# When a block's transposes and its expert stand between the products of the way out

## The chip, the cores and the metric

The kernel runs on one core of one Trainium2 chip. The metric is device time in microseconds (us) of one execution. Each core has five engines that run side by side, each through its own instructions in order: TensorE (PE, matrix products), VectorE (DVE), ScalarE (ACT), GpSimd (POOL) and SyncE (SP, which here only issues transfers). They wait for one another through semaphores. Products are written to PSUM, 8 banks of 2 KB per partition; everything else lies in SBUF or in device memory.

## The reference, cut to what matters

A transformer layer on 32 sequences of 64 tokens of width 512, in float32: cross attention to 256 context tokens, causal latent attention with 16 heads, and a feed-forward part. The change touches the end of the attention and one branch of the feed-forward:

```python
x = x + (heads @ wo.T + wo_b)                       # the way out of the attention
h = layernorm(x)
up = square(relu(h @ up_w)); shared = up @ down_w   # 512 -> 2048 -> 512
moe = (h @ expert_weight) * top2_sum(h @ gate_w)    # one expert, scaled per token
x = x + layernorm(shared + moe) * gamma + beta
```

## The kernel before

Every float32 operand is split into a high and a low part (`split`, L138 to L143: ACT casts the high part, DVE subtracts for the low part), and a product is made of three matmuls (high x high, low x high, high x low). The large products are, on top of that, tiled by a scheme with seven products in place of eight: sums of quarter blocks go in, seven products come out, and `combine` (L152 to L163) adds these into the result.

**The way out** (its loop is `for u, (blk, k) in enumerate(out_units)`, L1003 on) has 8 blocks of 256 tokens and 64 units. A unit is one block with one of 8 weight slots `k`: `seven` (L692 to L705) issues 21 matmuls of 128x256 on PE, into the block's four PSUM banks. Blocks 0 and 1 share the first 16 units. From block 2 on, block b has units 8b to 8b+7, so blocks 3, 4, 5, 6 end with units 31, 39, 47, 55, and block 7 with 63. The four banks of blocks 2 to 7 come from one pool with a single buffer; a block writes the banks that the block before it used.

What surrounds a unit:

- `left(u + 2)` splits the operand of the unit after next: an ACT cast (L141) and a DVE subtraction (L143), 128x896 each, from a piece `c` into one of three `hl` buffers. A buffer comes free when the unit three back is done on PE.
- `read_pair` (L666 to L681) fetches the pieces `c` by SP (L680), into three buffers.
- At a block's last unit `combine` runs: an ACT copy from bank 0 (L154), then on DVE L156 (bank 1), L158 and L159 (banks 2 and 0), L160 (bank 2) and L162 (bank 3). Their result `oo` has one buffer.
- `o_sum` (L920 to L929) adds the residual `ox` (L922) and takes the statistics (L926, L927); a power on POOL (L121) ends the norm's factor; `o_norm` applies it (L133) and yields `on`.
- `o_t` (L951 to L974), the block's **transposes**: 8 on PE (L959, tile `ops`), then casts on ACT (`oh`), subtractions on DVE (`ol`), copies `oT`, two stores `xT` issued by ACT (L971). Behind it `o_beta` (L945 to L949) adds beta to `oo` on DVE (L948) and stores it (`x2d`, by SP). Only then is the buffer `oo` free.
- `o_expert` (L976 to L998), the block's **expert**: 48 matmuls on PE (tile `cpe`, L173 to L175) into four banks of a pool of their own, the sum of the two largest gate values on DVE (L990, L992), the scaling on ACT (L995, L996) and a store `mo` issued by ACT.
- In the last eight units the first weights of the next stage are fetched (`cw_up`), cast and split (`wh_up`, `wl_up`; DVE 128x1024 and 128x768).

**What sets the order.** The kernel is written as one program; a scheduler then places each instruction on its engine, by costs and dependencies that it estimates, and may move an instruction past its neighbours (`issue_after` pins one behind another). Where a block's transposes and its expert are written is set by two tuples, L55 and L56: transposes of block i follow unit `TURN_AT[i]`, its expert follows unit `MULT_AT[i]`. The built order follows the tuples but for the ends, where matmuls trade places: after unit 23, for example, 17 of block 1's 48 expert products stand ahead of unit 24.

```python
TURN_AT = (19, 22, 28, 34, 42, 50, 58)
MULT_AT = (21, 25, 31, 39, 47, 55, 63)
...
        if u in TURN_AT:
            i = TURN_AT.index(u)
            xT[i] = o_t(i, xns.pop(i))
...
        if u in MULT_AT:
            i = MULT_AT.index(u)
            scaled = o_expert(i, *xT.pop(i))
```

Block 7's transposes and expert follow the loop. Before, the experts of blocks 2, 3, 4 and 5 thus stand behind the last units of blocks 3, 4, 5 and 6.

Of the kernel before, what the change touches and what calls it, by code (L numbers as in the profile page):

```python
# [51 lines left out]

SLOT_AT = (3, 5, 7, 9, 11)
EXPERT_AT = (15, 16, 17, 18)
TURN_AT = (19, 22, 28, 34, 42, 50, 58)  # L55
MULT_AT = (21, 25, 31, 39, 47, 55, 63)  # L56

BETA_AT = 60

# [20 lines left out]
def perceiver_block(ctx: ExitStack, tc: tile.TileContext, x, mem, mask, wq_a, bq_a, qnw, wq_b, bq_b,  # L80
# [97 lines left out]
    with ExitStack() as mla:  # L178
# [409 lines left out]
        with ExitStack() as pb:  # L588
# [46 lines left out]
            def load_slot(k, what):  # L635
                put_slot(k, what, read_slot(k, what))
# [308 lines left out]
    def o_beta(blk, pin=None):  # L945
        o2 = x2s.pop(blk)
        with after(pin):
            nc.vector.tensor_tensor(o2, o2, beb.unsqueeze(1).to_broadcast([P, 2, D]), ALU.add)  # L948
        nc.sync.dma_start(x2_d[blk], o2)  # L949

    def o_t(blk, xn, between=None):  # L951
        xT = ap.tile([P, NKD, TB], FP, tag="xn", name=f"oT{blk}")
        xh = ap.tile([P, NKD, TB], FR, tag="xh", name=f"oh{blk}")
        xl = ap.tile([P, NKD, TB], FR, tag="xl", name=f"ol{blk}")
        turned = []
        for tt in range(2):
            ps = ps_t.tile([P, NKD, P], FP, tag="T", name=f"ops{blk}_{tt}")
            for k in range(NKD):
                nc.tensor.transpose(ps[:, k, :], xn[:, tt, k * P : (k + 1) * P], ident)  # L959
            sl = slice(tt * P, (tt + 1) * P)  # L960
            low = split(xh[:, :, sl], xl[:, :, sl], ps)[1]
            if between:
                turned.append((sl, ps))
            else:
                copy = nc.scalar.copy(xT[:, :, sl], ps)
        if between:
            between()
        for sl, ps in turned:
            copy = nc.scalar.copy(xT[:, :, sl], ps)
        for i in range(2):  # L970
            nc.scalar.dma_start(xT_d[blk // 2][:, i, blk % 2], xT[:, 2 * i : 2 * i + 2, :])  # L971
        if blk > 1 and blk != NB - 2:
            o_beta(blk, low)
        return xh, xl, (copy, low)  # L974

    def o_expert(blk, xh, xl, _):  # L976

        mo = mos.pop(blk, None) or ap.tile([P, 2, D], FP, tag="mo", name=f"mo{blk}")
        for tt in range(2):
            i = 2 * blk + tt  # L980
            sl = slice(tt * P, (tt + 1) * P)
            pes = []
            for c in (slice(256, NE), slice(0, 256)):
                pe = ps_t.tile([P, D], FP, tag="T", name=f"cpe{i}_{c.start}")
                mm3(pe[:, 0 : c.stop - c.start], [
                    (xh[:, k, sl], xl[:, k, sl], wes[0][:, k, c], wes[1][:, k, c]) for k in range(NKD)
                ])
                pes.append(pe)
            t8 = sp.tile([P, 8], FP, tag="t8", name=f"t8{i}")
            nc.vector.max(t8, pes[0][:, 256:264])  # L990
            gs = sp.tile([P, 1], FP, tag="gs", name=f"gs{i}")
            nc.vector.tensor_tensor(gs, t8[:, 0:1], t8[:, 1:2], ALU.add)  # L992
            if tt:
                yield
            nc.scalar.mul(mo[:, tt, 256:512], pes[0][:, 0:256], gs)  # L995
            nc.scalar.mul(mo[:, tt, 0:256], pes[1][:, 0:256], gs)  # L996
        nc.scalar.dma_start(mo_d[blk], mo)
        yield  # L998
# [4 lines left out]
    for u, (blk, k) in enumerate(out_units):  # L1003
# [28 lines left out]
        if u - 8 * (NB - 1) in (0, 2, 4, 6):  # L1032
            load_slot(ORDER[(u % 8) // 2], "up")
# [3 lines that stand above are left out]
# [11 lines left out]
        if u == BETA_AT:  # L1048
            o_beta(NB - 2, low[1])
# [3 lines that stand above are left out]
# [327 lines left out]
```

## Time and profile before

| what | us |
|---|---|
| runs: median of three (lowest, highest) | 1113.07 (1111.52, 1113.95) |
| the profiled execution | 1114.92 |
| its span, first to last instruction | 1113.1 |
| PE busy in the span | 1069.7 |
| the way out's products, first to last | 554.9 to 765.2 |
| its transposes, first to last | 619.9 to 776.0 |
| its experts, first to last | 621.8 to 784.0 |

The page gives one execution. In its rows PE, DVE, ACT and POOL are the engines, PEld is the loading of weights into PE. A timeline row reads: start in us from the span's start, duration, engine, source line, operation, output<-input, and in brackets how long the engine was idle before it and what ended the wait. A row of the chain of waits has a start, a length and what the time went to. Rows of stretches give PE's busy time, its instructions, the clock granted to PE (1.00 is full speed), the busy share of the 16 DMA engines and what they moved.

### The profile page before, as it was taken

Reading aid. Unit: us, or ns where it says so; the run is one execution under the profiler, and the core shown is the slowest. Engines: PE = TensorE matmul, PEld = TensorE weight load, DVE = VectorE, ACT = ScalarE, POOL = GpSimd, SP = SyncE. Lnnn points to the kernel's source line nnn. Section 1 sums busy time; section 2 is a strip of 40 time slices with the busy share of each in tenths; the row PEclk is TensorE's granted clock in tenths of the full one; section 3 lists DMA queues with packets and bytes.
Section 4 is the critical chain, followed back from the end, with each engine's and each line's share of the span. In section 5 each row is a group of like instructions: output and inputs, shape, how many; then the busy total and the mean of one; then the engine's idle time right before and its main releaser. Section 6 shows DMA issues by size and latency. Waiting matters only on the chain.

```text
span 1113.1 us, 25983 instructions
## 1 busy us (share of the span) xinstructions
PE 1069.7 (96%) x10182; PEld 984.6 (88%) x10182; DVE 772.9 (69%) x1363; ACT 547.6 (49%) x1048; POOL 508.0 (46%) x694
## 2 busy tenths in 40 slices
PE   8899999999999999999989999998999998999896
PEld 6677777679999999999889999998999998999896
DVE  4666666647666667666878866668776577688796
ACT  4344444433444434433556544445676667564553
POOL 2333333326778777775471100002058770056761
PEclk9999999999999999999999999998999999999999
DMA  8777666343676787772498776776755789998681
GB/s 260 224 229 231 210 213 209 113 159 126 250 243 236 252 285 265 254 250 105 141 363 298 248 240 227 219 265 232 242 189 193 238 291 279 297 314 254 205 246 59
DMA packets 195386, 254.67 MB, mean 229 GB/s; under 512 B 18544, under 2 KB 140032, under 8 KB 195264
## 3 DMA queue, kind: packets, MB, share of 16 engines
q1 hardware_dynamic: 190848, 241.45, 66.1%
q10 hardware_dynamic: 3456, 8.39, 2.1%
q0 software_dynamic: 960, 3.18, 0.9%
q8 instruction: 80, 1.31, 0.5%
q14 instruction: 42, 0.34, 0.1%
HBM read 146.67 MB, written 106.30 MB: 227 GB/s over the span
## 4 chain that ended last, share of the span: by engine, by line
PE 59%; DMA 12%; DVE 11%; POOL 7%; issue 6%; ACT 4%; SPq 1%; DVEq 0%; POOLq 0%; ACTq 0%
PE up L1115 10%; PE pss L749 6%; PE psq L173 4%; PE psq L174 4%; PE psq L175 4%; PE psv L793 3%; PE op L702 2%; PE op L701 2%; PE op L699 2%; PE psc L367 2%; DMA cw_down<-wd_down 2%; DVE hl L143 2%; PE pse L173 2%; PE pse L175 2%; PE pse L174 2%
## 5 line engine op out<-in xcount | busy, mean ns | idle before, releaser
L731 DVE SCALAR_TENSOR_TENSOR qe<-pse,bqp,cq 64x256 f32<-64x256 f32 x256 | 123.8, 483 | 79.4 <-PE pse L175 73.3
L1115 PE MATMUL up<-xr,wh_up 128*128 128x256 f32 x896 | 154.8, 278 | 2.9 <-ACT up L154 2.9
L1115 PEld LDWEIGHTS up<-xr,wh_up 128*128 128x128 f32 x896 | 136.6, 190 | 3.1 <-ACT up L154 3.1
L701 PE MATMUL op<-wh_wo,hl 128*128 128x256 f32 x448 | 125.5, 280 | 4.8 <-DVE hl L143 4.7
L701 PE MATMUL dp<-wh_down,hl 128*128 128x256 f32 x448 | 124.9, 279 | 4.4 <-DVE hl L143 4.4
L143 DVE TENSOR_TENSOR hl<-c,hl 128x896 fp32r<-128x896 f32 x85 | 96.8, 1140 | 45.5 <-ACT hl L141 45.4
L699 PE MATMUL dp<-wh_down,hl 128*128 128x256 f32 x448 | 124.4, 278 | 1.5 <-DVE uo L159 1.5
L699 PE MATMUL op<-wh_wo,hl 128*128 128x256 f32 x448 | 125.5, 280 | 0.3 <-ACT hl L141 0.3
L702 PE MATMUL op<-wl_wo,hl 128*128 128x256 f32 x448 | 124.4, 278 | 0.1
L702 PE MATMUL dp<-wl_down,hl 128*128 128x256 f32 x448 | 124.4, 278 | 0.0
L1115 PE MATMUL up<-xr,wl_up 128*128 128x256 f32 x448 | 122.9, 278 | 0.0
L141 ACT CAST hl<-c 128x896 fp32r<-128x896 f32 x85 | 79.9, 943 | 76.0 <-PE op L702 33.2
L173 PE MATMUL psq<-qa_hi,qh 128*128 128x256 f32 x384 | 112.7, 294 | 0.0
L174 PE MATMUL psq<-qa_hi,ql 128*128 128x256 f32 x384 | 106.6, 278 | 0.0
L175 PE MATMUL psq<-qa_lo,qh 128*128 128x256 f32 x384 | 106.5, 277 | 0.0
L701 PEld LDWEIGHTS op<-wh_wo,hl 128*128 128x128 f32 x448 | 84.4, 188 | 6.5 <-DVE hl L143 6.4
L701 PEld LDWEIGHTS dp<-wh_down,hl 128*128 128x128 f32 x448 | 84.8, 189 | 5.1 <-DVE hl L143 5.0
L699 PEld LDWEIGHTS dp<-wh_down,hl 128*128 128x128 f32 x448 | 84.8, 189 | 1.7 <-issue 1.7
L699 PEld LDWEIGHTS op<-wh_wo,hl 128*128 128x128 f32 x448 | 84.2, 188 | 1.1 <-issue 0.7
L702 PEld LDWEIGHTS dp<-wl_down,hl 128*128 128x128 f32 x448 | 84.8, 189 | 0.0
L1115 PEld LDWEIGHTS up<-xr,wl_up 128*128 128x128 f32 x448 | 84.8, 189 | 0.0
L702 PEld LDWEIGHTS op<-wl_wo,hl 128*128 128x128 f32 x448 | 84.4, 189 | 0.3 <-DVE wl_wo L143 0.3
(227 smaller groups left out, 3152.8 us busy)
## 6 DMA issues: line engine op xcount, KB each, us to landing
c<-vd SPq DMA_DIRECT2D x58, 448.0 KB, 4.3
cx<-in_ctx SPq DMA_DIRECT2D x32, 512.0 KB, 4.6
vd<-vw SPq DMA_DIRECT2D x29, 512.0 KB, 3.8
hd<-uo SPq DMA_DIRECT2D x107, 128.0 KB, 3.4
hd<-uw SPq DMA_DIRECT2D x21, 512.0 KB, 3.0
dcw<-hd SPq DMA_DIRECT2D x18, 448.0 KB, 5.7
vd<-v SPq DMA_DIRECT2D x30, 256.0 KB, 3.3
c<-hd SPq DMA_DIRECT2D x17, 448.0 KB, 5.8
```

The source lines that it names most:

```text
L141: copy = nc.scalar.copy(hi, src)
L143: return copy, engine.tensor_tensor(lo, src, hi.bitcast(FP), ALU.subtract)
L173: nc.tensor.matmul(ps, ah, bh, start=(j == 0), stop=False)
L174: nc.tensor.matmul(ps, al, bh, start=False, stop=False)
L175: nc.tensor.matmul(ps, ah, bl, start=False, stop=(j == n - 1))
L699: first = nc.tensor.matmul(ps[s // 2][:, s % 2], h[:, a], wh[:, b], start=(k == 0 and s % 2 == 0), stop=False)
L701: nc.tensor.matmul(ps[s // 2][:, s % 2], l[:, a], wh[:, b], start=False, stop=False)
L702: ins = nc.tensor.matmul(ps[s // 2][:, s % 2], h[:, a], wl[:, b], start=False, stop=last)
L731: rope = nc.vector.scalar_tensor_tensor(qe[64 * a : 64 * a + 64, :], pe[r, :], bqp[r, p : p + 1], cq[r, a, :], ALU.add, ALU.mult,)
L749: nc.tensor.matmul(ps[64 * j : 64 * j + 64, pj, b, :], qs[2 * pj + j][a][:, sl], kT[:, a, kt], start=(a == 0), stop=(a == 1),)
L793: nc.tensor.matmul(o, kv[a, i, :], t[a, bp, :], start=True, stop=True)
L1115: nc.tensor.matmul(ps[s // 2][:, s % 2], w[:, i, kk], xr[b, 2 * kk + low][:, j], start=(first and m == 0), stop=(last and m == len(parts) ...
```

## The change

```diff
-TURN_AT = (19, 22, 28, 34, 42, 50, 58)
-MULT_AT = (21, 25, 31, 39, 47, 55, 63)
+TURN_AT = (19, 22, 28, 35, 43, 51, 58)
+MULT_AT = (21, 25, 30, 37, 45, 53, 63)
```

The transposes of blocks 3, 4 and 5 follow one unit later. The experts of blocks 3, 4 and 5 follow two units sooner, and that of block 2 one unit sooner. Between a block's transposes and its expert stand two units (for block 2: two in place of three; for blocks 3 to 5: two in place of five). No instruction is added, removed or resized. Blocks 0, 1, 6 and 7 keep their numbers, though the scheduler's order changes around block 6 too: in the built program its transposes stand 17 matmuls later, inside unit 59, and 4 of its 48 expert products stand ahead of the last products of block 7.

## The prediction

> **What bounds the kernel now.** First the page: TensorE (PE) is busy for 96% of the span.
>
> ```profile
> span 1113.1 us, 25983 instructions
> PE 1069.7 (96%) x10182; PEld 984.6 (88%) x10182; DVE 772.9 (69%) x1363; ACT 547.6 (49%) x1048; POOL 508.0 (46%) x694
> ```
>
> The change lies in the way out, whose products run from 554.9 to 765.2 us and whose experts end at 784. So next the busy time by stretches (length; PE busy and instructions; granted clock; DMA share; GB/s):
>
> ```profile
> 640.00:750.00 110.00, 110.00 (x945) 1.00 0.73 240
> 770.00:772.00 2.00, 1.26 (x11) 1.00 0.03 9
> 772.00:774.00 2.00, 0.00 (x0) 0.90 0.00 0
> 774.00:776.00 2.00, 1.54 (x8) 0.50 0.65 262
> ```
>
> Where the moved pairs stand, 640 to 750 us, PE never pauses: a product issues every 0.1135 us, a unit of 21 takes 2.385 us, an expert's 48 took 5.77 us (659.46 to 665.23). **No order of the same matmuls can gain there; it can only open gaps.** What can be lost shows in VectorE's (DVE) timeline at the end of block 4 (unit 39), where PE issued the block's last product at 685.51 and expert 3's first at 685.63:
>
> ```profile
> 684.91 1.09 DVE L143 TENSOR_TENSOR hl<-c,hl 128x896 fp32r<-128x896 f32 x1 [1.96 <-ACT hl L141]
> 685.92 0.68 DVE L156 TENSOR_TENSOR oo<-op,op 128x512 f32<-128x512 f32 x1
> 686.71 0.42 DVE L158 TENSOR_TENSOR oo<-oo,op 128x256 f32<-128x256 f32 x1
> 687.16 0.42 DVE L159 TENSOR_TENSOR oo<-oo,op 128x256 f32<-128x256 f32 x1
> 687.50 0.41 DVE L162 TENSOR_TENSOR oo<-oo,op 128x256 f32<-128x256 f32 x1
> 687.83 0.68 DVE L160 TENSOR_TENSOR oo<-oo,op 128x512 f32<-128x512 f32 x1
> ```
>
> These five sums read the block's four PSUM banks, and the next block writes the same four (their pool has one buffer): bank 1 is free after L156, bank 0 after L159, bank 3 after L162, bank 2 after L160. They end 3.0 us after the block's last product, and nobody waits: PE is in the expert, whose banks are others, until 691.4. **The expert behind a block's last unit is the cover of its combine.** The last view is the chain of waits at the end of the stage:
>
> ```profile
> 759.72 1.23 DVE oo L948
> 760.95 0.02 issue
> 760.97 5.82 DMA x2d<-oo
> ...
> 766.91 0.70 DVE oo L156
> ...
> 773.38 0.94 DVE on L133
> 774.33 0.14 issue
> ```
>
> Block 7's combine waits until block 6's sum, in the single buffer `oo`, is stored; its norm ends the last transposes' wait. PE idles 3.2 us up to 774.46 and then runs at granted clock 0.50 to about 780.4 (rows of 2 us further on show 0.89 from 780 to 782): 6.0 us at half speed, 3.0 us lost.
>
> **The change, part by part.** Nothing is added or removed: the 48 products of three experts (blocks 3 to 5, 144 in all) move two units up, block 2's 48 one unit up, and 8 transposes x 3 blocks (3 to 5) one unit down. Moved work costs nothing itself. What it issues moves along: ScalarE's (ACT) store of `mo` comes earlier, its two stores of `xT` one unit later; both are read far later. On SyncE's queue the built order has the read of a block's second piece `c` ahead of the `x2d` store instead of behind, and `ox` one place later; the next to need `ox` is a whole block away (25 us).
>
> *Cover lost at four block ends.* In the new order nothing stands on PE between the last unit of blocks 3, 4, 5, 6 and the next block's first product; the built order starts these on bank 1, then 0, 3, 2: the order in which combine frees them. Blocks 4 to 6, counted from T, the slot after the block's last product: the piece cast ahead of L156 starts when the unit before is done, 0.20 after the slot that follows it (667.82 against 667.62), so at T - 2.18; its DVE half starts 0.98 later (667.82 to 668.80), T - 1.20; L156 1.01 later (684.91 to 685.92), T - 0.19; it takes 0.68, PE wakes 0.05 later (569.43 + 1.08 to 570.56), and the first pair after a wait costs 0.11 more (570.56 to 570.78): **0.65 us of gap**. L159 starts 1.24 after L156 and ends at T + 1.47, when PE is still on bank 1 (9 products, to T + 1.7). Bank 0 costs nothing, the others follow.
>
> The trace has no block end without cover, so bounds from the nearest rows, T to the end of L156: 686.60 - 685.63 = 0.97 at block 4; block 2, whose next block came 17 expert products later, 635.03 - 633.29 = 1.74; block 6, 740.76 - 737.97 = 2.79; below, 0, if the cast is early. The large ones have a cause: the cast ahead of L156 had waited for its read (idle before it 2.11 us at 683.93 and 2.58 at 738.09, put down to DMA `c`). In the new order that read leaves ahead of the store, and 5.77 us of expert stand between its issue and its need. I take 0.65 and keep 0 and 2.8.
>
> At block 3 the built order puts the cast of unit 34 between L158 and L159, and it needs unit 31 done: ACT at T + 0.20, DVE T + 1.18 to 2.27, PE again 0.05 + 0.11 later; PE has 13 products (1.47 us) until it needs it: 0.95. Sum: 0.95 + 3 x 0.65 = **2.9 us**.
>
> *Block 6's queue.* With block 5's expert gone from behind unit 55, DVE meets the burst and the `up` weights together. From L156 at T - 0.19, by starts in the rows: L160 at 1.72, a cast 2.32, L922 3.32, first `wl_up` 4.47, two L926 to 6.82, second `wl_up` to 7.9, then the cast of unit 59, whose end is 9.04. PE gets there at 0.65 + 3 x 2.385 + 4 products = 8.25: 0.95 with the restart. Block 6's norm, now behind one more cast, then holds its transposes about 0.25. In the same units PE lost 0.43 + 0.16 + 0.60 = 1.2 us before (steps at 757.3, 759.9, 762.9); I leave that as it is, plus 0.15. Sum: **1.35 us**; ends 0 and 2.5 (twice the 1.2).
>
> *The end of the stage.* The build now has 4 of block 6's expert products ahead of the last unit, so PE reaches its last product later: 4 x 0.117 = 0.47. The beta sum L948 moves behind one more `wl_up` (0.87), and its store behind one more 512 KB read on SyncE (at the 339 to 430 GB/s of these slices 1.2 to 1.5). Before, the store landed at 766.79, 1.46 after the last product's next slot (765.33); now 0.9 to 2.3 later. I take 1.6. With the 0.47 this is **2.1 us**; from 0.5, if it lands under other DVE work, to 4. PE's idle time before the last transposes becomes some 5 us, and the half-speed stretch after it I leave at 3.0; half as long or half again as long, it would give 1.5 back or take 1.5.
>
> The total: 2.9 + 1.35 + 2.1 = +6.35 us. The profiled execution took 1114.92 us (span 1113.1, 1.8 around it), so its like would be 1121.3; it lies 1.85 above the median of the runs, 1113.07, to which the same difference gives **1119.4 us**.
>
> The trace has PE waits of 0.59 to 1.32 us between 570 and 590 with the clock at 1.00, so I charge no clock for the new gaps. A rule speaks otherwise. The Trainium skill, page "TensorE: Matmul & The Clock Gate", section "A second HAM failure mode: psum-queue depth-cycling", tells of a kernel whose short PE pauses at every change of PSUM banks made the clock swing between half and full. By that rule each of the four block ends could bring one 3.41 us window (the page's figure) at half rate, an estimate of 4 x 1.7 = 6.8 us more, 1126.2.
>
> **The rivals.**
> 1. *Late reads stay late*: each block end costs the 2.8 of block 6 and not 0.65 or 0.95. For it: the DMA share of 0.73, and idle times before casts that end on `c`. Against: the read now has an expert's time more. 4 x 2.8 - 2.9 = 8.3 more: 1127.7. Half of it, 1123.6, is likelier than all.
> 2. *The cover is not needed*: the casts run ahead, L156 ends before T, and DVE's burst at block 6 finds gaps. For it: DVE idles 31%. Against: a cast can't start before a buffer is free, and only three exist. Then only the 0.47 and some of the store: +1, 1114.1.
> 3. *Faster*: block 6's store gets out early. If `x2d` is issued before about 758.9 and not at 760.97, L156 starts 1.9 sooner, PE's idle time falls to the 1.3 us that left the clock alone at 570, and 3.0 of half clock go; with the 1.2 us of units 59 to 63 that is 6.1 less, against 2.9 more for the block ends: 1109.9. Against: the built order puts this store later on both of its queues.
>
> **How the numbers follow.** A measurement of this kernel tells 0.2% (2.2 us) from no change. Forecast, +4 to +9: 0.60. Only part of it, +2.2 to +4: 0.13. Late reads or clock, over +9: 0.15. Rival 2, within 2.2: 0.09. Rival 3: 0.03. So slower 0.88. The range from +2.4 to +11.9, 1115.5 to 1125.0, leaves out the two last cases and the far half of the late reads.
>
> **What will show it.** In the PE waits: three of about 0.5 us on `oo` L156 at block ends and one of about 0.9 on a cast (L143) 1.5 us after block 3's end; none in the expert or at the transposes of blocks 3 to 5. At unit 59 a wait on L143 of about 1 us. The chain's `x2d` piece again 5 to 7 us long, L156 2.5 to 4 us behind the last product and PE idle 4.5 to 6 us before the last transposes. I am wrong if PE stays gapless from 640 to 750, if the waits end on DMA `c`, or if the clock falls below 1.00 before the last transposes.

## The result, and the profile after

| | median of the runs, us (lowest, highest) | profiled execution | its span |
|---|---|---|---|
| before, 22 runs | 1113.58 (1108.51, 1117.92) | 1114.92 | 1113.1 |
| after, 22 runs | 1116.72 (1113.31, 1123.17) | 1113.31 | 1111.5 |

The ratio of all runs is 1.0035, with a 95% interval of 1.002 to 1.005: the change makes the kernel slower by 3.9 us (2.2 to 5.6); the two medians lie 3.1 us apart. The prediction was 1119.4 in a range of 1115.5 to 1125.0, so the sign and the range held, and the size was too large: the measured loss lies just below the main case (+4 to +9, 0.60), in the one that had 0.13.

One profile misleads here. The profiled execution after is shorter than the one before, although the kernel is slower: single executions scatter by some 10 us, and a profile is one of them. So I read the changed stage and not the span. First the page of the kernel after, its top lines:

```profile
span 1111.5 us, 25986 instructions
PE 1068.6 (96%) x10182; PEld 983.2 (88%) x10182; DVE 771.7 (69%) x1363; ACT 547.1 (49%) x1048; POOL 507.4 (46%) x694
```

The totals tell nothing: the work is the same. The stretch in which PE never paused before now has pauses, at a full clock. These rows show five engines, each with its busy time and instructions (PE, PEld, DVE, ACT, POOL), then the clock, the DMA share and GB/s:

```profile
640.00:750.00 110.00, 108.33 (x927) 107.52 (x926) 69.66 (x114) 49.22 (x73) 2.76 (x4) 1.00 0.71 232
```

Which they are, PE's waits in that stretch after say (what PE waits for; total us, times, longest us). The same view of before has no line at all:

```profile
PE op L699 <- DVE oo L156: 1.1, 3, 0.4
PE op L701 <- DVE hl L143: 0.5, 1, 0.5
```

The three waits on L156 are at the ends of blocks 4, 5 and 6, the one on a cast 1.6 us after block 3's end (664.5). The end of block 4 in VectorE's timeline of after; the last column is the idle time before an instruction and what ended it:

```profile
690.19 1.09 DVE L143 TENSOR_TENSOR hl<-c,hl 128x896 fp32r<-128x896 f32 x1 [4.42 <-ACT hl L141]
691.20 0.68 DVE L156 TENSOR_TENSOR oo<-op,op 128x512 f32<-128x512 f32 x1
691.99 0.42 DVE L158 TENSOR_TENSOR oo<-oo,op 128x256 f32<-128x256 f32 x1
692.44 0.42 DVE L159 TENSOR_TENSOR oo<-oo,op 128x256 f32<-128x256 f32 x1
```

And PE's timeline of the same place:

```profile
691.29 0.28 PE L702 MATMUL op<-wl_wo,hl 128*128 128x256 f32 x1
691.94 0.39 PE L699 MATMUL op<-wh_wo,hl 128*128 128x256 f32 x1 [0.38 <-DVE oo L156]
692.16 0.28 PE L701 MATMUL op<-wh_wo,hl 128*128 128x256 f32 x1
```

Block 4's last product issues at 691.29, so the next slot is 691.40. Block 5's first product waits for bank 1, which L156 leaves at 691.88, and issues at 691.94, 0.54 late; the next one takes 0.22 instead of 0.11. Together **0.65 us of gap**. The list of waits shows less (0.38), because it counts from the modelled end of the last product, not from the missed slot. L156 starts 0.20 before the slot; before, at the same place, it started 0.29 behind it (685.92 against 685.63), and nobody saw it, since 5.77 us of expert stood there.

The other half of the result is the end of the stage, in the chain of waits of after:

```profile
763.27 1.23 DVE oo L948
764.52 3.85 DMA x2d<-oo
768.50 0.70 DVE oo L156
...
774.97 0.94 DVE on L133
775.91 0.14 issue
776.05 0.64 PE ops L959 x4
```

The beta sum is 3.55 us later than before. Of this, 2.33 us are those by which the last product is later; against that product the sum is 1.22 us later, as its later place foretold, but the store takes 3.85 us and not 5.82. It lands at 768.37, 0.72 behind the slot after the last product (767.65); before it was 1.46. PE idles 2.95 us before the last transposes (3.19 before), and in this profile the half-speed stretch behind it is shorter too:

```profile
776.00:778.00 2.00, 1.57 (x10) 1.14 (x10) 1.44 (x2) 1.01 (x2) 2.00 (x3) 0.97 0.43 172
778.00:780.00 2.00, 1.93 (x8) 1.93 (x9) 1.82 (x3) 1.73 (x4) 2.00 (x4) 0.50 0.04 8
780.00:782.00 2.00, 2.00 (x13) 2.00 (x13) 1.57 (x4) 1.27 (x2) 1.79 (x2) 0.68 0.79 293
```

### The profile page after: what moved, and what is told of

The parts are those of the page before. It is cut to its first block, busy times and chain, and to the rows that moved or that the text cites. A ratio compares the mean times of both kernels' runs of the same rounds, so it can differ in the third digit from the quotient of the medians.

```text
span 1111.5 us, 25986 instructions
## 1 busy us (share of the span) xinstructions
PE 1068.6 (96%) x10182; PEld 983.2 (88%) x10182; DVE 771.7 (69%) x1363; ACT 547.1 (49%) x1048; POOL 507.4 (46%) x694
```

## The experiments

**The theories.** C, the cover: what costs is that no expert stands behind a block's last unit, so PE meets the combine. D, the distance: what costs is that only two units lie between a block's transposes and its expert, so that casts, stores and norms of one block are packed together. A smaller question went along: whether the later transposes are harmless, and what sets the end of the stage.

So that the runs can be compared, each profiled execution is cut in two, by PE's timeline: the *queue*, from the first product behind block 1's expert to block 7's last product (798 products, 40 transposes, four experts; in after, e2, e4, e5 and e6 also 4 products of the fifth, 0.5 us, and in e11 12, 1.5 us), and the *tail*, from there to block 7's first transpose. The ratio has its own runs of the kernel before on the same chip beside it.

| kernel | waits at ends of blocks 3, 4, 5, 6, us | queue | tail | ratio (interval) |
|---|---|---|---|---|
| before | none | 121.20 | 9.25 | 1 |
| after | 0.54, 0.38, 0.38, 0.38 | 124.15 | 8.51 | 1.0035 (1.002 to 1.005) |
| e1 transposes alone | none | 119.74 | 9.08 | 1.0003 (0.9986 to 1.0021) |
| e2 experts alone | 0.54, 0.38, 0.38, 0.38 | 127.05 | 8.83 | 1.0066 (1.004 to 1.0093) |
| e4 one expert alone | block 6: 0.38 | 122.60 | 8.66 | 1.0026 (1.0009 to 1.0043) |
| e10 all but that expert | 0.58, 0.38, 0.38, none | 123.58 | 9.21 | 1.0024 (1.0006 to 1.0042) |
| e3 two units, all late | none, none, 0.18, 3.76 | 125.50 | 8.31 | 1.0049 (1.0029 to 1.0069) |
| e9 two units, but block 5 | none, none, 0.30, none | 121.40 | 8.87 | 1.0012 (0.9988 to 1.0035) |
| e7 half an expert as cover | none | 120.93 | 8.88 | 1.0004 (0.9988 to 1.002) |
| e5 fewer PSUM banks | as after | 125.04 | 8.85 | 1.0047 (1.0025 to 1.0069) |
| e6 a second bank 1 | 0.69, 0.20, 0.21, 0.20 | 124.05 | 9.63 | 1.0046 (1.0028 to 1.0064) |
| e8 e1, earlier store | none | 120.50 | 7.57 | 0.999 (0.9974 to 1.0007) |
| e11 after, earlier store | as after | 125.26 | 6.91 | 1.003 (1.001 to 1.0051) |
| e12 e8, last sums by halves | none | 120.19 | 6.92 | 1.0 (0.9982 to 1.0018) |

The ratios go with the queue, and hardly with the tail. The five kernels that can't be told from before (e1, e7, e8, e9, e12) have a queue of 119.74 to 121.40, 120.55 on average, so the 121.20 of before's own profile may be a slow one; after's queue lies 2.95 above the one and 3.6 above the other.

**e1 and e2: the halves of the change.** e1:

```diff
-TURN_AT = (19, 22, 28, 34, 42, 50, 58)
+TURN_AT = (19, 22, 28, 35, 43, 51, 58)
```

> Only the transposes of blocks 3 to 5 one unit later; the experts stay behind the blocks' last units, four units behind their transposes. Theory C (cover: what costs is that no expert stands between a block's last product and the next block's first): no PE wait on the combine (L156) at any block end, time within 1 us of the kernel before. Rival D (distance: what costs is that transposes and expert lie close together, so that their casts and scalings crowd ACT and DVE): one unit of the three that were taken away is gone, so about a third of the change's +3.9 us, +1.3 us.

Ratio 1.0003: the later transposes alone cost nothing that can be measured, and there is no wait from 640 us to block 7. e2:

```diff
-MULT_AT = (21, 25, 31, 39, 47, 55, 63)
+MULT_AT = (21, 25, 30, 37, 45, 53, 63)
```

> Only the experts sooner; the transposes stay where they were, so three units lie between. Theory C: the same four gaps at the ends of blocks 3 to 6 (one on the cast L143, three on L156 of about 0.4 us) and the pile-up at unit 59, so at least the change's +3.9 us; on top, block 3 to 5's norms are late by then, because their statistics queue behind casts of a block that started earlier: three waits of the transposes on L133 of about 1 us each, so +5 to +9 us over before. Rival D: three units between instead of two, so slower than before by less than the change, about +2.6 us, and no waits at block ends that the change did not have.

Ratio 1.0066, more than the whole change, though the two intervals overlap. PE's waits of e2 from 640 to 750 us:

```profile
PE ops L959 <- DVE on L133: 2.8, 3, 0.9
PE op L699 <- DVE oo L156: 1.1, 3, 0.4
PE op L701 <- DVE hl L143: 0.5, 1, 0.5
```

The last two lines are those of after: the experts bring them, whatever the transposes do. The first line is new. Without an expert behind a block's end the next units come 5.77 us sooner, and the transposes that follow the third of them now wait for their norm. In the whole change the transposes stand one unit later, and these 2.8 us are not there. **So the change is a loss in its experts and a repair in its transposes.**

**e4 and e10: one block end by itself.** e4 moves block 5's expert alone, e10 all but that one.

```diff
-MULT_AT = (21, 25, 31, 39, 47, 55, 63)
+MULT_AT = (21, 25, 31, 39, 47, 53, 63)
```

> Only block 5's expert is moved, from behind unit 55 to behind unit 53; everything else as before. Theory C: of the change's cost just the last block end's part: one wait on L156 of 0.4 us behind unit 55, the wait of unit 59 on a cast (L143) of about 0.6 us and of block 6's transposes of 0.4 us, and in exchange the waits at units 61 and 63 (0.16 and 0.33 us) gone: +1 to +3 us. If the four block ends each cost a quarter: +1.0 us and no wait at unit 59.

```diff
-TURN_AT = (19, 22, 28, 34, 42, 50, 58)
-MULT_AT = (21, 25, 31, 39, 47, 55, 63)
+TURN_AT = (19, 22, 28, 35, 43, 51, 58)
+MULT_AT = (21, 25, 30, 37, 45, 55, 63)
```

> The changed kernel with block 5's expert left behind unit 55. Theory C: block ends 3, 4 and 5 keep their waits (one on L143 of 0.55 us, two on L156 of 0.38), block 6's end and unit 59 have none, and block 6's transposes do not wait: +1 to +2 us over before, the change less the +2.9 us of the kernel with block 5's expert alone moved. If the four ends cost alike: +2.9 us.

In e4 the wait on L156 stands at the end of block 6 and nowhere else, and the ratio is 1.0026; in e10 there is a wait at all ends but that one, ratio 1.0024. Each wait at a block end follows its expert. One point of e10's expectation failed: at unit 59, where none was to be, PE waits 1.05 us for a cast (753.28), and the loss is 2.7 us and not 1 to 2. The two costs add to 1.005, the whole change has 1.0035: within their intervals, the same.

**e3 and e9: two units between, with the cover kept.** Experts as before, transposes drawn up to two units ahead of them. e3:

```diff
-TURN_AT = (19, 22, 28, 34, 42, 50, 58)
+TURN_AT = (19, 22, 29, 37, 45, 53, 58)
```

> Two units between transposes and expert for blocks 2 to 5 as in the change, but reached by moving the transposes later (after units 29, 37, 45, 53); the experts stay behind the blocks' last units. Theory C: no wait on L156 at block ends, time within 1.5 us of before. Rival D: two units between, so the change's +3.9 us.

The ratio, 1.0049, is what D asked for, but the trace is not: no wait at the ends of blocks 3 and 4, one of 0.18 us at the end of block 5, one of 3.76 us at the end of block 6. The chain of e3 there, then PE's timeline:

```profile
735.86 1.23 DVE oo L948
737.09 0.02 issue
737.10 8.59 DMA x2d<-oo
...
745.78 0.69 DVE oo L156
...
747.10 0.38 ACT mo L996
```

```profile
747.53 0.43 PE L699 MATMUL op<-wh_wo,hl 128*128 128x256 f32 x1 [3.76 <-ACT mo L996]
747.76 0.42 PE L701 MATMUL op<-wh_wo,hl 128*128 128x256 f32 x1
```

This is a third cause. Transposes so late put the beta sum behind them late, its store took 8.59 us, and until it has landed the one buffer `oo` can't take block 6's sums. L156 waited 4.3 us, the expert's scaling (L992, L995, L996) stood behind it, and the products behind that issue 0.21 us apart instead of 0.11, at half clock. So e9 leaves block 5's transposes at their old place:

```diff
-TURN_AT = (19, 22, 28, 34, 42, 50, 58)
+TURN_AT = (19, 22, 29, 37, 45, 50, 58)
```

> As the kernel with two units between by later transposes, but block 5 is left as it was (transposes after 50, expert after 55), since there a store of oo came too late and held PE for 3.8 us. Blocks 2 to 4 still have two units between. Theory C, with the store as the cause of that kernel's loss: no wait at any block end, from one expert's start to the next 26.2 us or a little less, time within 1 us of before. Rival D: three of the four close pairs stay, so about 3 us of the change's 3.9.

Its only wait from 640 to 750 us:

```profile
PE op L699 <- ACT mo L996: 0.3, 1, 0.3
```

Ratio 1.0012, no clear difference, with two units between for blocks 2, 3 and 4. The 0.3 us is e3's mechanism in small: block 4's store (711.45, 5.59 us) ends at 717.04 and L156 behind it. The ratio alone doesn't settle D: its interval still holds the 3 us that D asked for. The trace does: from one block's last product to the next block's, e9 takes 25.89 us for blocks 4 and 5, before 26.17. And e2, with three units between, lost 4.4 to 10.3 us where D asked for 2.6. **D falls**: two units between cost nothing while an expert stands at the block's end and the store is not late.

**e7: how much cover is needed.** The change, but with each of the four moved experts cut in two: 24 products at the new place, 24 behind the block's end. In `o_expert`, between the two token halves, and in the loop:

```diff
+            if tt:
+                yield
...
-            if i < NB - 2:
+            if not 2 <= i < NB - 2:
+                next(scaled)
+            if i < 2:
                 next(scaled)
+        if u in (31, 39, 47, 55):
+            next(scaled)
+            next(scaled)
```

> The changed kernel with each expert of blocks 2 to 5 cut in two: the first 128 tokens' 24 products where the change has the whole, the second 24 behind the block's last unit, as cover. Theory C: 24 products are 2.9 us, more than the 0.5 us that PE waited for L156 and the 1.5 us that the last bank needs, so no wait on L156 at any block end and no wait on L143 at block 3's; some of the crowding at block 6 stays. +0.5 to +2 us over before, so 2 to 3 us less than the change. If a whole expert is needed as cover, the waits stay, shorter.

No wait at any block end, and the ratio is 1.0004: 24 products, 2.9 us, hide a combine whose first bank comes free 0.5 us late and whose last 3.0 us after the block. This is the strongest evidence for C, since the transposes and the first half of each moved expert stay where the change has them.

**e5 and e6: another bank in place of cover.** If PE waits for bank 1 because it is the same bank, a second bank 1 must take the wait away. It has to come from the pool of the transposes and experts: e5 takes that bank away and uses it for nothing, e6 gives it to every second block.

```diff
-                ps_t = pc.enter_context(pool("o_pst", 4, space=PSUM))
+                ps_t = pc.enter_context(pool("o_pst", 3, space=PSUM))
```

> The changed kernel with three PSUM banks in place of four for the transposes and the experts; it is the control for the next kernel. Theory C: the same waits as in the change (three on L156 of about 0.4 us at the ends of blocks 4, 5, 6, one on L143 at block 3's), and a new wait of the last expert on its scaling (L996), about 2 us, because its fourth tile has no bank: +2 us over the change, +6 over before.

```diff
-    def banks(pool, nm):
+    def banks(pool, nm, one=None):
-        return [pool.tile([P, 2, TB], FP, tag=f"p{i}", name=f"{nm}_{i}") for i in range(4)]
+        return [(one if one and i == 1 else pool).tile([P, 2, TB], FP, tag=f"p{i}", name=f"{nm}_{i}") for i in range(4)]
...
-            pss[blk] = banks(ps_p, f"op{blk}")
+            pss[blk] = banks(ps_p, f"op{blk}", ps_x if blk % 2 else None)
...
-                ps_t = pc.enter_context(pool("o_pst", 4, space=PSUM))
+                ps_t = pc.enter_context(pool("o_pst", 3, space=PSUM))
+                ps_x = pc.enter_context(pool("o_psx", space=PSUM))
```

> As the kernel before it in this list, but the bank that this frees is given to bank 1 of every second block (3, 5, 7), so that a block's first products need not wait for the block before to be summed. Theory C: the three waits on L156 vanish, and with each the restart after it; the waits on L143 (block 3's end, unit 59) stay. 1.5 to 2.5 us less than with three banks alone. If the gaps at block ends came from late operands (reads of c, casts) and not from the banks, they would stay and so would the time.

PE's timeline of e6 at the same block end:

```profile
691.83 0.28 PE L701 MATMUL op<-wh_wo,hl 128*128 128x256 f32 x1
692.31 0.36 PE L699 MATMUL op<-wh_wo,hl 128*128 128x256 f32 x1 [0.20 <-DVE oo L159]
```

The waits on L156 are gone, and a wait on L159, for bank 0, stands in their place. So the cause of the wait is the bank; but a block's end costs only 0.23 us less than in after and not the whole gap (15.07 us against 15.30 for the 126 products around block 4's end), and the time is that of e5, 1.0046 against 1.0047: the expectation of a gain in the time failed. e6's queue is 1.0 us shorter than e5's, but its tail is 0.8 us longer: there the last expert waits 1.23 us for its scaling, in e5 0.46 (about 2 were expected). Sums that end one behind the other release one bank after another; taking the first wait away shows the second.

**e8, e11 and e12: the end of the stage.** e8 is e1 with block 6's beta sum and store ordered behind unit 58.

```diff
-BETA_AT = 60
+BETA_AT = 58
```

> The transposes of blocks 3 to 5 one unit later (which alone changed nothing) and block 6's beta sum (L948) written two units sooner, so that its store of oo leaves before the next weights' splits. If the wait of the last combine on this store sets the end of the stage: no wait on DMA x2d ahead of the last L156, its start 0.8 to 1 us sooner after the last product, the idle time before the last transposes 2.2 us in place of 3.0 to 3.2, and 1 to 2.5 us less than before (more where the half-clock stretch goes as well). If DVE's own queue (the splits of the up weights) sets it: no change.

In e8 the store is out of the chain, L156 runs right behind the last product (762.99 against 762.95), and PE idles 1.54 us before the last transposes, not 3.02 as in e1. The tail is 1.5 us shorter (the queue is 0.8 us longer, with a wait of 0.74 us on a cast at 755.91 that e1 does not have), and the clock is not halved behind it, as two stretches of e8 show:

```profile
770.00:772.00 2.00, 1.24 (x9) 1.01 (x10) 1.44 (x3) 0.58 (x1) 2.00 (x4) 1.00 0.66 262
772.00:774.00 2.00, 1.78 (x15) 1.57 (x15) 1.82 (x3) 1.68 (x4) 2.00 (x4) 1.00 0.03 8
```

And yet the time is 1.1 us less than before, with an interval of -2.9 to +0.8: not told from no change. e11 is the same edit on the kernel after:

> The whole change, and block 6's beta sum with its store ordered behind unit 58 in place of 60. Theory C (cover) puts +3.3 us into the block ends and block 6's queue and lets the end of the stage be set by the store x2d of block 6 alone: the three waits of 0.38 us on oo L156 and the two on casts stay, the store lands before the last product, the idle time ahead of the last transposes falls from 2.95 to 1.5 us (as with the earlier store in the run e8), and the time stands at +2 to +3 us against before, ratio 1.002 to 1.003. If the tail were set by something other than that store, idle time there stays at 3 us and the ratio at 1.0035.

The waits at the block ends are unchanged, and so is the ratio, 1.003. The tail falls by 1.6 us, but the queue rises by 1.1: the scheduler drew 12 of block 6's expert products ahead of the last unit and not 4, and these are 1.0 us that only changed sides. PE idles 2.35 us and not the expected 1.5, since block 7's L156 is now held by DVE's own queue (769.37, behind a `wl_up` that began at 767.20) and not by the store. e12 adds to e8 that block 7's residual sum and statistics are done by halves:

```diff
-            nc.vector.tensor_tensor(o2, o2, xt, ALU.add)
...
+        if blk == NB - 1:
+            mrs = []
+            for tt in range(2):
+                nc.vector.tensor_tensor(o2[:, tt], o2[:, tt], xt[:, tt], ALU.add)
+                mrs.append(ln_stats(sp, o2[:, tt], 1e-5, f"o{blk}_{tt}"))
+            return o2, mrs
```

> Transposes of the change, experts of before, the store x2d of block 6 behind unit 58, and block 7's residual sum and statistics done by halves of 128 tokens, so that the factor of the first half is ready before the second half is summed. Theory C: no wait at a block end, as in e1 and e8. The idle time ahead of the last transposes, 3.0 to 3.2 us before and 1.54 in e8, falls by the length of one half's sum and statistics, some 1.2 us, to 0.3 to 0.8 us; the half-clock stretch of 3.4 us or more after it may go with it (1.7 us). Against before -1.5 to -4 us, ratio 0.9965 to 0.9985. If the clock falls all the same, ratio 0.998 to 0.9995.

PE's timeline of e12 from block 7's transposes on (L965 is L959 of before; the edit adds six lines above it):

```profile
770.89 0.63 PE L965 MATMUL ops<-ident,on 128*128 128x128 f32 x4 [0.88 <-DVE on L133]
771.81 0.63 PE L965 MATMUL ops<-ident,on 128*128 128x128 f32 x4 [0.29 <-DVE on L133]
773.73 0.50 PE L173 MATMUL cpe<-we_hi,oh 128*128 128x264 f32 x2 [1.29 <-ACT oh L141]
```

The idle time falls to 0.88 us, close to the 0.3 to 0.8 expected, and a new one of 1.29 us follows: the cast of the transposes queues behind the scaling of block 6's expert on ScalarE. The clock is halved for a stretch all the same. Ratio 1.0. No kernel of this study is clearly faster than before.

## Why the prediction was right, and where its sizes failed

*Block ends, 2.9 us.* The mechanism held step by step, and the gaps too: 0.65 at the ends of blocks 4, 5 and 6 as worked out, 0.81 at block 3 (predicted 0.95; 666.03 to 666.85, less one slot, and 0.11 of restart). That is 2.76 gross.

*What the gaps take back.* By PE's segments, experts aside, the queue grew by 1.4 us up to block 6's last product, where the gaps of the ends of blocks 3 to 5 are 2.11, and by 1.03 from there to block 7's last product, where the gaps are 0.65 at the block end, 0.87 at unit 59 (predicted 0.95) and 0.44 at block 6's transposes (predicted 0.25). In the first place the 0.7 us comes from products that already ran slower in before: 105 products behind a block's transposes took 12.45 us, where 105 x 0.1135 is 11.92. In after a part of these products runs at the faster pace. I had called this stretch gapless and the unit 2.385 us. In the second, 0.9 us comes from what units 59 to 63 lost before (105 products in 13.64 us, 1.7 over their pace; the prediction had 1.2 of it), which I left in place "as it is": once PE has waited at unit 59 and at the transposes, only some 0.5 us is lost behind these places. **In this trace the new lateness took the place of the old and did not add to it**; I had added the two. It is no rule: e10 waits 1.05 us at unit 59 and again 0.35 us at 763.89.

*End of the stage, 2.1 us.* The 0.47 for the expert's products is there: 0.52, in two pieces. The 1.6 us for the store failed: measured -0.74. Against the last product the beta sum was 1.22 us later (predicted 0.87), and one more read stood ahead of the store, as the orders of the queues said; but the store took 3.85 us where I had kept some 5 to 7. What goes with it is how far the reads ahead of it still were: in both kernels the store lands 1.27 us behind the last of them, a piece `xp`, and this landed 4.55 us behind the store's issue before and 2.58 us after. A read further ahead, `cw_up`, took 7.9 us before and was still under way; after, it took 4.8 us and had landed. The reads behind the store explain less: in after, e4 and e6 they are issued alike, 0.4 and 3.0 us behind it, and the store took 3.85, 3.96 and 4.93 us. This was compared, not tried by itself, and why the reads were sooner done is open. L156 thus starts 0.96 us behind the last product (768.50), not 2.5 to 4, the idle time of 5 us never came, and the half-speed stretch, which I had left at 3.0 us lost, was shorter in after's profile: about 3.4 us long and not 6.8 (PE ran in 6.0 of these). Other profiles have the longer stretch behind a shorter idle time and the shorter one behind a longer (last section), so this may be chance.

*The sum.* Predicted +6.35; by the traces' stage 2.95 of queue - 0.74 of tail = +2.2, by the runs +3.9 (2.2 to 5.6). The term that failed is the store's, 2.3 us too large; the queue terms, 4.7 predicted, measured 2.95 to 3.6. Both errors have the same sign, so the range held by its width; the sign of the result held by the mechanism.

*The rivals.* Late reads did not stay late: the cast ahead of L156 waits 4.42 us at 690.19, and the ScalarE half before it ended its wait on PE (the buffer), not on the read. "The cover is not needed" fell by the waits of after, e2, e4 and e10 and by e7. "Faster" had the right mechanism in the wrong place: a store that leaves early shortens the tail (e8), but this change did not send it early. As for the clock, the granted clock stayed at 1.00 from 640 to 750 us with four pauses of 0.4 to 0.5 us in it. The Trainium skill ("TensorE: Matmul & The Clock Gate", "A second HAM failure mode: psum-queue depth-cycling") tells of pauses at bank changes that come often enough to swing the clock; pauses this short, one per 26 us, did not in this profile, and the 6.8 us estimated from that page did not come.

*What stays open.* The runs' 3.9 us stand against the 2.2 of two single profiles (1.6 if the stage is counted to the end of the experts, where the shorter half-speed stretch counts too). Before's profile may lie high in the queue, but one profile for each kernel can't show it: between the last products of blocks 6 and 7, kernels with the same order of products there take 26.17 (e1), 26.62 (e12), 26.92 (e8), 27.36 (before), 27.40 (e9) and 28.13 us (e10).

## What to carry to other kernels

Where an accumulation group has only one set of PSUM banks, look at what stands on TensorE between its last matmul and the next group's first: work on other banks there is the cover of the combine, a few us of it are enough (half an expert did as well as a whole), and moving it away costs a gap at every group, worked out from one DVE row. When two tuples move together, run each alone: here one half was the loss and the other repaired a wait that the first had made. And believe a ratio only when the trace has the wait that the theory names: e3 had D's number and another cause.

## What was not expected of the hardware

- PE's products have two steady paces at a granted clock of 1.00, about 0.1135 and about 0.1176 us each. Before, they run at the first behind an expert's matmuls and at the second behind transposes (105 in 12.45 us, less the start), until the next expert. That is no rule: in after the 42 products behind the transposes of block 4 take 4.87 us, the first pace, those behind the transposes of block 3 5.03 us, the second; and behind a wait on a PSUM bank the second pace follows at block 4's end and the first at block 5's. In e7, with half an expert at the block's end, the 84 products behind it take 9.55 us, 0.1137 each. Why is not settled.
- A store of `oo`, 512 KB each time, took 3.85, 5.82 and 8.59 us in three kernels of this study; it landed 1.27, 1.27 and 1.39 us behind the last read that SyncE had issued ahead of it.
- Idle PE ahead of block 7's transposes, one profile for each kernel: behind 1.54 us (e8) the clock stayed at 1.00; behind 2.35 (e11), 2.95 (after) and 3.27 us (e2) it was halved for about 3.4 us, behind 2.83 (e9) and 3.19 us (before) for about 6.8. So the length of the idle time does not give that of the half-speed stretch. In e12 it was halved behind pauses of 0.88, 0.29 and 1.29 us that follow one another within 4 us, while pauses of 0.4 to 0.6 us left it at 1.00 from 640 to 756 us in after. And the waits of the first units, which the prediction took as harmless since before has 0.59 to 1.32 us there at 1.00, are not always so: in e8, behind 0.41 and 1.17 us, the clock was halved from about 582 to 585.5 us.
